# Deferred last tile between target groups of the graph attention loop, and rows B and C of the state space stage fetched in one transfer

## The chip, the cores and the metric

The kernel runs on one core of one Trainium2 chip. The metric is device microseconds of that core from start to end of one execution; "before" is the median of three runs. A profiled execution gives the trace that is read below. Engines are TensorE (PE, with its weight loads PEld), VectorE (DVE), ScalarE (ACT), GpSimd (POOL) and SyncE (SP), which only issues transfers.

## The reference, cut to what matters

Four layers of a graph network on 3125 nodes with 256 features. Layers 1 and 2 each hold a graph attention network of two attention layers; layer 3 holds one, and beside it a state space model (Mamba) over the nodes in sorted order. Of all this the change touches two parts. The second attention layer of layers 1 and 2 (and, of layer 1, the first too) is

```python
h = (x @ W).reshape(n, heads, out_ch)
e = leaky_relu(alpha_src[src] + alpha_dst[dst], 0.2)
m = segment_max(e, dst)
e = exp(e - m[dst])
alpha = e / segment_sum(e, dst)[dst]
out = segment_sum(alpha[:, :, None] * h[src], dst)
```

and its result, plus a bias, is added to x and normed over the features for the feed-forward part that follows. The state space model is a recurrence over the nodes with 16 states for each of 256 channels:

```python
dbc = xc @ x_proj_w.T                    # 16 values for dt, then rows B (16), then rows C (16)
dt = softplus(dbc[:, :16] @ dt_proj_w.T + dt_proj_b)
dA = exp(dt[:, :, None] * A);  dBx = (dt * xc)[:, :, None] * B[:, None, :]
h = dA_t * h + dBx_t                     # one step for each node t
y_t = h @ C_t
```

## The kernel before, in words

Nodes lie in 25 tiles of 125 (P) on the partitions. The program is written in a tile framework: the code says what is computed in which program order, the framework orders each engine's instructions by its own estimate of when their inputs are ready, and puts in the waits. So the code's order is a strong hint and not a list. [...]

**Attention.** `gat` (L1050) chooses between two ways; on these inputs `gat_products` (L1070) runs. It takes the targets in 5 groups (NG) of 5 tiles (GB). For a group, `spread` (L168) lays a factor of the targets along the free dimension: one-column transposes on TensorE into PSUM, copied out by ScalarE or VectorE (L78, L80). Then it goes over the 25 source tiles: a block of the dense adjacency is loaded by SyncE (`load_edges`), VectorE forms the weights `t` (L1124, one instruction for each head, three buffers), and TensorE adds `t`-block times `h` into one PSUM accumulator for each target tile and head (L1129). After the last source it calls `use` for each of the 5 target tiles in turn (L1132 and L1133) and runs it through before the next group's spreads are issued.

`use` is a generator of the caller. In `gat_last` (L1310; one head, width 256; layers 1 and 2) it is `use2`: divide by the sum of weights (`shares`, L1217: L1234, L1236, L1247 on VectorE), two additions on GpSimd (L1321, L1322), and after the fifth tile of a group the norm of all five (`centred`, L1799: statistics and a reciprocal root on VectorE with one step on ScalarE, then five scalings on ScalarE, L1806) and their turn (`turn`, L144: ten transposes on TensorE at L149 with four copies out on ScalarE at L151). In `gat_heads` (L1274; four heads) it is `use1`: shares, bias, ELU, transposes of the tile (L1299), copy out, a product with the next weights (L166), copies out. With width 128 (layer 1) `gat_heads` uses this loop too, with 7 PSUM banks for the accumulators and 1 for everything else. With width 64 (layers 2 and 3) another loop, `sums_by_feature`, runs, which the change leaves alone.

**State space.** `l3_mamba` (L1931) takes groups of four tiles (500 nodes), six of them and one of a single tile. `first_part` of a group makes xc, dt and u = dt * xc, and rows B and C. It is a generator, advanced one step for each state of the group before. A second generator, `beside`, runs layer 3's mixer (`l3_mix`), one step for each of the first nine states of a group. `recur(s)` handles state s for 128 channels at a time (c = 0, 1): the decay on ScalarE into PSUM (L2059), u times row B on VectorE (L2060), the scan along the nodes on VectorE (L2061), the last column kept on ScalarE (L2063), times row C on GpSimd (L2064). `add` sums the 16 states on TensorE with the identity (L2070); its buffer `bx` has four copies. Row B reaches the 128 partitions by a matmul (L2052): the 32 rows of B and C are split into three bfloat16 parts (`b1`, `b2`, `bc`; L2030 to L2038) and a one-column selection, broadcast, times them gives row s on all partitions, in PSUM. Row C comes by a transfer issued from ScalarE's queue: all C rows are written once for each group to DRAM (`crows`, L2033), and for each state one row is read back onto 128 partitions (L2049, three buffers).

Of the kernel before, what the change touches and what calls it, by code (L numbers as in the profile page):

```python
# [11 lines left out]
F32 = mybir.dt.float32  # L12
# [48 lines left out]
class Net:  # L61
# [1008 lines left out]
    def gat_products(self, far, h, al, heads, width, loops, use):  # L1070
# [3 lines left out]
        with ExitStack() as es:  # L1074
# [23 lines left out]
            cp = es.enter_context(self.pool("gq_acc", 1, PSUM))  # L1098
            pp = es.enter_context(self.pool("gq_ps", min(2, 8 - banks), PSUM))
            for g in range(NG):  # L1100
                rows = lp.tile([P, heads, GW], F32, name="rows")
# [14 lines left out]
                for s in range(NT):  # L1116
# [9 lines left out]
                    for b in range(GB):  # L1126
                        for hd in range(heads):
                            first = (b * heads + hd) % per == 0
                            nc.tensor.matmul(acc(b, hd), t[:, hd, b * P:(b + 1) * P], h[:, s, hd, :],  # L1129
                                             start=(s == 0 and first), stop=(s == NT - 1),  # L1130
                                             skip_group_check=True)
# [799 lines left out]
    def l3_mamba(self, xs, ys, beside):  # L1931
# [6 lines left out]
        with ExitStack() as es:  # L1938
# [20 lines left out]
            nc.vector.memset(state, 0.0)  # L1959

            wbc = wp.tile([128, KC, 3, 2 * S], F32, name="wbc")
            nc.vector.tensor_copy(wbc, wx[:, :, None, S:].to_broadcast([128, KC, 3, 2 * S]))
            pick = wp.tile([6 * S, 2 * S], BF16, name="pick")
            rest = wp.tile([6 * S, 2], F32, name="rest")
            for k in range(3):
                ks = slice(k * 2 * S, (k + 1) * 2 * S)
                nc.vector.tensor_copy(pick[ks], self.ident[ks, ks])
                for c in range(2):
                    nc.vector.memset(rest[ks, c:c + 1], float(k > c))
            crows = self.dram.tile([S, N], F32, name="crows")  # L1970
            last = wp.tile([128, KC, 3], F32, name="last")
            nc.vector.memset(last, 0.0)

            def first_part(g, n, into):
# [42 lines left out]
                for c in range(KC):  # L2017
# [8 lines left out]
                b1 = kp.tile([6 * S, 4 * P], BF16, name="b1", tag="b", bufs=1)  # L2026
                r1 = kp.tile([6 * S, 4 * P], F32, name="r1", bufs=1)
                b2 = kp.tile([6 * S, 4 * P], BF16, name="b2", tag="b", bufs=1)
                bc = kp.tile([6 * S, 4 * P], BF16, name="bc")
# [12 lines left out]
                nc.gpsimd.tensor_mul(u[:, :, :w], dt[:, :, :w], xc[:, :, :w])  # L2042
                into += [sz, xc, bc, dt, u]

            def recur(s, g, w, bc, dt, u):
# [6 lines left out]
                nc.tensor.matmul(bps[:, :w], pick[:, s:s + 1].to_broadcast([6 * S, 128]), bc[:, :w],  # L2052
                                 start=True, stop=True)
                out = []
                for c in range(KC):
# [3 lines left out]
                    nc.scalar.activation(da[:, :w], dt[:, c, :w], AF.Exp, scale=an[:, c, s:s + 1])  # L2059
                    nc.vector.tensor_mul(bx[:, :w], u[:, c, :w], bps[:, :w])  # L2060
                    nc.vector.tensor_tensor_scan(h[:, :w], da[:, :w], bx[:, :w], state[:, c, s:s + 1],  # L2061
# [28 lines left out]
            for k, (g, n) in enumerate(GROUPS):  # L2090
                w = n * P
                sz, xc, bc, dt, u = now
# [3 lines left out]
                terms = [recur(0, g, w, bc, dt, u)]  # L2096
                if done:
                    next(done)
                for s in range(S):
                    if s + 1 < S:  # L2100
                        terms.append(recur(s + 1, g, w, bc, dt, u))
                    if s:
# [21 lines left out]
    def l3_gnn(self):  # L2124
# [420 lines left out]
```

## Time and profile before

| what | us |
|---|---|
| median of three runs | 7015.29 (7009.70 to 7022.92) |
| profiled execution | 7013.64 |
| its span in the trace | 7011.9 |
| stretch with `gat_heads` of layer 1 | about 1781 to 2480 |
| stretch with `gat_last` of layer 1 | about 2480 to 2850 |
| stretch with `gat_last` of layer 2 | about 4375 to 4765 |
| stretch of the state space stage | about 5118 to 5826 |

Over the whole span TensorE is busy 85%, VectorE 53%, ScalarE 23%, GpSimd 13%. These are averages over stages with different limits, so the views below are taken by stage. A row of groups ends with the idle time just ahead of the group on its engine and the instruction that ended most of it. A row of the timeline has the start, the length, the engine, the line and the operation, and in brackets the idle time before it. A row of waits has the total, the number of times and the longest. In a table of stretches each engine has its busy time, then come the granted TensorE clock as a share of full speed, the share of the DMA engines and GB/s.

### The profile page before, as it was taken

Reading aid. Unit: us, or ns where it says so; the run is one execution under the profiler, and the core shown is the slowest. Engines: PE = TensorE matmul, PEld = TensorE weight load, DVE = VectorE, ACT = ScalarE, POOL = GpSimd, SP = SyncE. Lnnn points to the kernel's source line nnn. Section 1 sums busy time; section 2 is a strip of 40 time slices with the busy share of each in tenths; the row PEclk is TensorE's granted clock in tenths of the full one; section 3 lists DMA queues with packets and bytes.
Section 4 is the critical chain, followed back from the end, with each engine's and each line's share of the span. In section 5 each row is a group of like instructions: output and inputs, shape, how many; then the busy total and the mean of one; then the engine's idle time right before and its main releaser. Section 6 shows DMA issues by size and latency. Waiting matters only on the chain. (4 is left out here: it accounts for less than half of the span.)

```text
span 7011.9 us, 78426 instructions
## 1 busy us (share of the span) xinstructions
PE 5946.1 (85%) x29487; PEld 3981.8 (57%) x29487; DVE 3714.8 (53%) x7628; ACT 1603.4 (23%) x3404; POOL 885.3 (13%) x685
## 2 busy tenths in 40 slices
PE   6887999996799987899946999789878887998875
PEld 5555775664799966658843344676534333333543
DVE  7644123227776643215036887446377777776523
ACT  2423002331100010113313011001256661003411
POOL 0000000004000001400041000101324442001111
PEclk7978999998999998889977999898889998998887
DMA  2724447301122133315520322440232213222042
GB/s 67 109 40 71 129 133 229 98 9 61 53 62 60 53 105 102 92 50 174 174 59 15 82 78 55 114 115 9 79 40 55 58 45 89 65 70 75 31 120 79
DMA packets 421339, 562.00 MB, mean 80 GB/s; under 512 B 120485, under 2 KB 307169, under 8 KB 417153
## 3 DMA queue, kind: packets, MB, share of 16 engines
q1 hardware_dynamic: 353687, 458.72, 25.3%
q10 hardware_dynamic: 40467, 70.52, 3.7%
q0 software_dynamic: 26752, 27.20, 1.5%
q8 instruction: 247, 4.05, 0.2%
q14 instruction: 186, 1.52, 0.1%
HBM read 446.41 MB, written 109.65 MB: 79 GB/s over the span
## 5 line engine op out<-in xcount | busy, mean ns | idle before, releaser
L1124 DVE SCALAR_TENSOR_TENSOR t<-rows,over,a 125x625 f32<-125x625 f32 x750 | 617.4, 867 | 424.1 <-PE acc L1129 421.5
L1190 DVE SCALAR_TENSOR_TENSOR t<-rows,over,a 125x750 f32<-125x750 f32 (+1 forms) x800 | 795.0, 1045 | 57.8 <-PE acc L1204 53.3
L1195 PE MATMUL acc<-t,g_h 125*64 125x375 f32 (+1 forms) x3200 | 625.8, 500 | 12.2 <-DVE t L1190 12.2
L1129 PE MATMUL acc<-h,t 125*125 125x257 f32 x2500 | 566.4, 391 | 28.5 <-DVE t L1124 20.2
L1129 PE MATMUL acc<-g_h,t 125*125 125x129 f32 x5000 | 565.7, 275 | 1.3 <-DVE t L1124 1.1
L1129 PEld LDWEIGHTS acc<-g_h,t 125*125 125x125 f32 x5000 | 562.4, 189 | 3.2 <-DVE t L1124 2.9
L1129 PEld LDWEIGHTS acc<-h,t 125*125 125x125 f32 x2500 | 483.2, 194 | 110.5 <-issue 17.5
L1195 PEld LDWEIGHTS acc<-t,g_h 125*64 125x64 f32 x3200 | 226.9, 136 | 356.2 <-issue 247.0
L1204 PE MATMUL acc<-t,g_h 125*32 125x375 f32 (+1 forms) x3200 | 377.4, 497 | 0.0
L2064 POOL TENSOR_TENSOR bx<-h,crow 128x500 f32<-128x500 f32 (+1 forms) x224 | 270.6, 1223 | 343.1 <-DVE h L2061 107.2
L2070 PE MATMUL y<-bx,ident 128*128 128x500 f32 (+1 forms) x448 | 242.3, 650 | 76.7 <-POOL bx L2064 74.4
L771 PE MATMUL agg<-h,a 125*125 125x257 f32 x1250 | 278.0, 383 | 13.9 <-DMA a<-adj 8.7
L837 DVE SCALAR_TENSOR_TENSOR X<-ps_out,prob,X 125x256 f32<-125x256 f32 x200 | 87.9, 480 | 357.3 <-PE ps_out L166 357.1
L771 PEld LDWEIGHTS agg<-h,a 125*125 125x125 f32 x1250 | 233.4, 188 | 56.8 <-issue 18.1
L149 PE MATMUL ps_turn<-ident,XN 125*128 125x125 f32 x300 | 70.7, 386 | 223.9 <-DVE XN L138 109.8
L2061 DVE TENSOR_TENSOR_SCAN h<-da,state,bx 128x500 f32<-128x500 f32 (+1 forms) x224 | 246.9, 1130 | 20.7 <-ACT da L2059 17.8
L1204 PEld LDWEIGHTS acc<-t,g_h 125*32 125x32 f32 x3200 | 104.1, 109 | 249.6 <-issue 248.7
L563 ACT ACTIVATE h<-ps_hidden,L_ffn_b,bn_s 128x500 f32<-128x500 f32 (+1 forms) x224 | 160.6, 722 | 355.1 <-PE ps_hidden L166 330.7
L166 PE MATMUL ps_hidden<-xbt,w 128*128 128x250 f32 x928 | 204.6, 378 | 16.2 <-ACT xbt L151 16.2
L166 PE MATMUL ps_out<-w,hb 128*125 128x256 f32 x928 | 205.0, 379 | 0.0
L166 PE MATMUL ps_hidden<-XNT,L_ffn_W 128*128 128x500 f32 (+1 forms) x448 | 199.2, 569 | 0.0
L166 PEld LDWEIGHTS ps_hidden<-xbt,w 128*128 128x128 f32 x928 | 174.5, 191 | 41.9 <-ACT xbt L151 23.1
(724 smaller groups left out, 9477.3 us busy)
## 6 DMA issues: line engine op xcount, KB each, us to landing
a<-adj SPq DMA_DIRECT2D x500, 273.4 KB
a<-adj SPq DMA_DIRECT2D x150, 328.1 KB
arow<-adj SPq DMA_DIRECT2D x25, 1367.2 KB
adj<-block SPq DMA_DIRECT2D x22, 1531.2 KB
w<-in_L_ffn_W1p SPq DMA_DIRECT2D x29, 1024.0 KB
w<-in_L_ffn_W2p SPq DMA_DIRECT2D x29, 1024.0 KB
crow<-crows ACTq DMA_DIRECT2D x96, 250.0 KB
a<-adj SPq DMA_DIRECT2D x50, 382.8 KB
```

What stands on the lines that cost most here:

```text
L166: self.nc.tensor.matmul(ps, lhsT[k], rhs[k], start=(k == 0), stop=(k == n - 1))
L563: self.nc.scalar.activation(out[:, f, :], ps[:, :nt], func, **kw)
L771: nc.tensor.matmul(acc[b][:P, :D + 1], a[:, b * P:(b + 1) * P], h[:, s, :], start=(s == 0), stop=(s == NT - 1))
L837: nc.vector.scalar_tensor_tensor(x, ps, prob[:, g + j, e:e + 1], x, op0=ALU.mult, op1=ALU.add)
L1124: nc.vector.scalar_tensor_tensor(t[:, hd, :], rows[:, hd, :], over[:, s, hd:hd + 1], a, op0=ALU.max, op1=ALU.mult)
L1129: nc.tensor.matmul(acc(b, hd), t[:, hd, b * P:(b + 1) * P], h[:, s, hd, :], start=(s == 0 and first), stop=(s == NT - 1), skip_group_check ...
L1190: nc.vector.scalar_tensor_tensor(t[hd][:, :w], rows[hd][:, :w], over[:, s, hd:hd + 1], a[:, :w], op0=ALU.max, op1=ALU.mult)
L1195: nc.tensor.matmul(acc[k][c][q * width:(q + 1) * width, :c1 - c0], h[:, s, 2 * k + q, :width], t[2 * k + q][:, c0:c1], start=(s == 0), sto ...
L1204: nc.tensor.matmul(acc[pairs][c][hd * 32:(hd + 1) * 32, :c1 - c0], h[:, s1, hd, width:].to_broadcast([P, 32]), t1[hd][:, c0:c1], start=(s1 ...
L2061: nc.vector.tensor_tensor_scan(h[:, :w], da[:, :w], bx[:, :w], state[:, c, s:s + 1], op0=ALU.mult, op1=ALU.add)
L2064: nc.gpsimd.tensor_mul(bx[:, :w], h[:, :w], crow[:, :w])
L2070: nc.tensor.matmul(acc[c][:, :w], self.ident, terms[c][:, :w], start=(s == 0), stop=(s == S - 1))
```

## The change

In `gat_products` the `use` of a group's last tile is run only to its first yield; its remaining steps are taken one after every fourth source of the next group, and what is left is run before that group's own tiles. `use2` gets two yields, so its steps are: shares and additions; the norm; the first turn (three tiles); the second turn (two tiles). `use1` had its yields already (within the ELU, and between the copy out and the product).

In `l3_mamba` the rows B and C are computed once in float32, written together to DRAM as 32 rows (`bc_rows`), and for each state one transfer brings row B and row C onto 128 partitions. The split into bfloat16 parts, the selection tiles and the matmul for row B go. The PSUM pool of this function has one buffer in place of two, and the mixer's, `m3_ps`, three in place of two. Lines of the new kernel that answer to the old: L1125 to L1124, L1130 to L1129, L2037 to L2049, L2045 to L2059, L2046 to L2060, L2047 to L2061, L2049 to L2063, L2050 to L2064, L2056 to L2070.

```diff
@@ gat_products
+            later = iter(())
             for g in range(NG):
...
+                    if s % 4 == 3 and later:
+                        next(later, None)
+                self.through(later)
                 for b in range(GB):
-                    self.through(use(pp, g * GB + b, parts(b), None))
+                    later = use(pp, g * GB + b, parts(b), None)
+                    next(later, None)
+                    if b < GB - 1:
+                        self.through(later)
+            self.through(later)
@@ gat_last, use2
                 nc.gpsimd.tensor_add(self.X[:, i, :], self.X[:, i, :], x)
+                yield
                 if i % GB == GB - 1:
                     g = i - GB + 1
                     self.centred(kp, xn[:, g:g + GB, :], self.X[:, g:g + GB, :], GB, "li")
                     for b0, n in ((0, 3), (3, 2)):
+                        yield
                         self.turn(pp, xnt[:, :, (g + b0) * P:(g + b0 + n) * P], xn[:, g + b0:g + b0 + n, :], n,
                                   evac=nc.scalar.copy)
@@ l3_mamba
-            pp = es.enter_context(self.pool("mb_ps", 2, PSUM))
+            pp = es.enter_context(self.pool("mb_ps", 1, PSUM))
...
-            crows = self.dram.tile([S, N], F32, name="crows")
+            rows = self.dram.tile([2 * S, N], F32, name="bc_rows")
@@ l3_mamba, first_part
-                self.product(ps[:6 * S, :w], [wbc[:, c].rearrange("p k s -> p (k s)") for c in range(KC)],
-                             [xc[:, c, :w] for c in range(KC)])
...
-                nc.scalar.copy(b1[:, :w], ps[:6 * S, :w])
+                self.product(ps[:2 * S, :w], [wx[:, c, S:] for c in range(KC)], [xc[:, c, :w] for c in range(KC)])
                 both = kp.tile([2 * S, 4 * P], F32, name="both", tag="low", bufs=1)
                 nc.scalar.copy(both[:, :w], ps[:2 * S, :w])
-                nc.scalar.dma_start(crows[:, g * P:g * P + w], both[S:, :w])
-                nc.vector.scalar_tensor_tensor(r1[:, :w], b1[:, :w], rest[:, 0:1], ps[:6 * S, :w],
-                                               op0=ALU.mult, op1=ALU.subtract)
+                nc.scalar.dma_start(rows[:, g * P:g * P + w], both[:, :w])
                 yield
-                nc.scalar.copy(b2[:, :w], r1[:, :w])
-                nc.vector.scalar_tensor_tensor(bc[:, :w], b2[:, :w], rest[:, 1:2], r1[:, :w],
-                                               op0=ALU.mult, op1=ALU.subtract)
@@ l3_mamba, recur
-                crow = vp.tile([128, 4 * P], F32, name="crow")
-                row = crows[s:s + 1, g * P:g * P + w]
-                nc.scalar.dma_start(crow[:, :w], bass.AP(tensor=row.tensor, offset=row.offset,
-                                                         ap=[[0, 128], [1, w]]))
-                bps = pp.tile([128, 512], F32, name="ps_b", tag="mm")
-                nc.tensor.matmul(bps[:, :w], pick[:, s:s + 1].to_broadcast([6 * S, 128]), bc[:, :w],
-                                 start=True, stop=True)
+                both = vp.tile([128, 2, 4 * P], F32, name="both")
+                row = rows[s:s + 1, g * P:g * P + w]
+                nc.scalar.dma_start(both[:, :, :w], bass.AP(tensor=row.tensor, offset=row.offset,
+                                                            ap=[[0, 128], [S * N, 2], [1, w]]))
+                brow, crow = both[:, 0, :], both[:, 1, :]
...
-                    nc.vector.tensor_mul(bx[:, :w], u[:, c, :w], bps[:, :w])
+                    nc.vector.tensor_mul(bx[:, :w], u[:, c, :w], brow[:, :w])
@@ l3_gnn
-                pp = es.enter_context(self.pool("m3_ps", 2, PSUM))
+                pp = es.enter_context(self.pool("m3_ps", 3, PSUM))
```

More of the change, by code (lines that the diff above doesn't have):

```diff
@@ L1959, in l3_mamba @@
             nc.vector.memset(state, 0.0)
[L1961 to L1969, printed above, removed]
-            crows = self.dram.tile([S, N], F32, name="crows")
+            rows = self.dram.tile([2 * S, N], F32, name="bc_rows")
             last = wp.tile([128, KC, 3], F32, name="last")
@@ L2023, in first_part @@
                 ps = pp.tile([128, 512], F32, name="ps_dbc", tag="mm")
-                self.product(ps[:6 * S, :w], [wbc[:, c].rearrange("p k s -> p (k s)") for c in range(KC)],
-                             [xc[:, c, :w] for c in range(KC)])
[L2026 to L2029, printed above, removed]
-                nc.scalar.copy(b1[:, :w], ps[:6 * S, :w])
+                self.product(ps[:2 * S, :w], [wx[:, c, S:] for c in range(KC)], [xc[:, c, :w] for c in range(KC)])
                 both = kp.tile([2 * S, 4 * P], F32, name="both", tag="low", bufs=1)
                 nc.scalar.copy(both[:, :w], ps[:2 * S, :w])
-                nc.scalar.dma_start(crows[:, g * P:g * P + w], both[S:, :w])
-                nc.vector.scalar_tensor_tensor(r1[:, :w], b1[:, :w], rest[:, 0:1], ps[:6 * S, :w],
-                                               op0=ALU.mult, op1=ALU.subtract)
+                nc.scalar.dma_start(rows[:, g * P:g * P + w], both[:, :w])
                 yield
-                nc.scalar.copy(b2[:, :w], r1[:, :w])
-                nc.vector.scalar_tensor_tensor(bc[:, :w], b2[:, :w], rest[:, 1:2], r1[:, :w],
-                                               op0=ALU.mult, op1=ALU.subtract)
                 yield from self.softplus(fp, dt[:, :, :w], dt[:, :, :w])
@@ L2042, in first_part, with recur @@
                 nc.gpsimd.tensor_mul(u[:, :, :w], dt[:, :, :w], xc[:, :, :w])
-                into += [sz, xc, bc, dt, u]
-            def recur(s, g, w, bc, dt, u):
-                crow = vp.tile([128, 4 * P], F32, name="crow")
-                row = crows[s:s + 1, g * P:g * P + w]
-                nc.scalar.dma_start(crow[:, :w], bass.AP(tensor=row.tensor, offset=row.offset,
-                                                         ap=[[0, 128], [1, w]]))
-                bps = pp.tile([128, 512], F32, name="ps_b", tag="mm")
-                nc.tensor.matmul(bps[:, :w], pick[:, s:s + 1].to_broadcast([6 * S, 128]), bc[:, :w],
-                                 start=True, stop=True)
+                into += [sz, xc, dt, u]
+            def recur(s, g, w, dt, u):
+                both = vp.tile([128, 2, 4 * P], F32, name="both")
[3 more added lines that the diff above has]
+                brow, crow = both[:, 0, :], both[:, 1, :]
                 out = []
@@ L2091, in l3_mamba @@
                 w = n * P
-                sz, xc, bc, dt, u = now
+                sz, xc, dt, u = now
                 now = []
@@ L2095, in l3_mamba @@
                 acc = [cp.tile([128, 512], F32, name=f"y{c}") for c in range(KC)]
-                terms = [recur(0, g, w, bc, dt, u)]
+                terms = [recur(0, g, w, dt, u)]
                 if done:
@@ L2100, in l3_mamba @@
                     if s + 1 < S:
-                        terms.append(recur(s + 1, g, w, bc, dt, u))
+                        terms.append(recur(s + 1, g, w, dt, u))
                     if s:
```

## The prediction

> **What bounds the kernel now.** The change touches two kinds of stage, so I read each stage by itself: first the costliest groups (line, engine, operation, tile, count | busy us, mean ns | idle before, and who ended it).
>
> ```profile
> L1124 DVE SCALAR_TENSOR_TENSOR t<-rows,over,a 125x625 f32<-125x625 f32 x750 | 617.4, 867 | 424.1 <-PE acc L1129 421.5
> L1129 PE MATMUL acc<-h,t 125*125 125x257 f32 x2500 | 566.4, 391 | 28.5 <-DVE t L1124 20.2
> ```
>
> In the source loop of `gat_products` VectorE waits for TensorE (421.5 us), hardly the reverse: TensorE sets the pace. Its own holes lie between groups of targets. The timeline of TensorE about one boundary in `gat_last` of layer 1:
>
> ```profile
> 2689.72 11.22 PE L1129 MATMUL acc<-h,t 125*125 125x257 f32 x51
> 2710.74 1.66 PE L149 MATMUL ps_turn<-ident,XN 125*128 125x125 f32 x6 [9.80 <-ACT XN L1806]
> 2713.06 1.09 PE L149 MATMUL ps_turn<-ident,XN 125*128 125x125 f32 x4 [0.66 <-ACT XNT L151]
> 2714.20 1.41 PE L174 MATMUL ps_spread<-ident,mine 125*125 125x125 f32 x5
> 2717.08 3.36 PE L1129 MATMUL acc<-h,t 125*125 125x257 f32 x7 [1.47 <-DVE t L1124]
> ```
>
> The products end at 2700.94 and start again at 2717.08: a hole of 16.1 us, nearly all of it the norm of the five tiles (9.80 us of waiting) and their turns. The other boundaries of both `gat_last` stages show the same within 0.3 us. The products also come back slow. The stretches table (us, busy of PE, PEld, DVE, ACT, POOL, granted clock, DMA):
>
> ```profile
> 2717.00:2722.00 5.00, 4.92 (x12) 3.87 (x13) 1.82 (x4) 0.00 (x0) 0.00 (x0) 0.50 0.68 188
> ```
>
> One source takes 2.17 us in steady state (VectorE's next `t` starts every 2.17 us); the first after the hole takes 4.69 (2717.08 to 2721.77). So a hole costs about 2.5 us more.
>
> The state space stage runs from about 5118 to 5822. Its waits (us in total, times, longest) and four stretches:
>
> ```profile
> PEld y L2070 <- POOL bx L2064: 157.1, 121, 4.1
> POOL bx L2064 <- DVE h L2061: 107.1, 38, 12.4
> DVE bx L2060 <- PE ps_b L2052: 67.6, 22, 16.7
> ```
> ```profile
> 5300.00:5310.00 10.00, 10.00 (x29) 5.12 (x28) 4.51 (x6) 4.15 (x10) 2.20 (x2) 1.00 0.18 51
> 5310.00:5320.00 10.00, 10.00 (x38) 6.79 (x37) 5.26 (x12) 6.50 (x12) 1.97 (x3) 1.00 0.07 26
> 5340.00:5350.00 10.00, 7.62 (x27) 3.59 (x26) 10.00 (x14) 6.05 (x12) 5.78 (x4) 1.00 0.22 45
> 5350.00:5360.00 10.00, 6.54 (x18) 2.89 (x18) 10.00 (x10) 6.00 (x13) 4.08 (x3) 0.91 0.16 46
> ```
>
> A group of four tiles (some 105 us) has two halves: first TensorE is full with the mixer that runs beside it and VectorE waits for row B, which stands in TensorE's queue; then VectorE is full. By the scans' starts, some 43 of the 96 steps of full width (one state each) take under 5.3 us, the shortest 3.47: there VectorE is the bound. The rest take longer.
>
> **What the Trainium skill says.** "SBUF — State Buffer", Who interferes with whom: VectorE with two inputs in SBUF and a GpSimd instruction that reads SBUF exclude each other for a whole instruction; an input in PSUM takes VectorE out of this. The trace agrees:
>
> ```profile
> 5457.23 3.39 POOL L2064 TENSOR_TENSOR bx<-h,crow 128x500 f32<-128x500 f32 x2 [1.35 <-DVE h L2061]
> ```
> ```profile
> 5458.18 1.35 DVE L1926 SCALAR_TENSOR_TENSOR sp_l<-sp_w,sp_l 128x1000 f32<-128x1000 f32 x1
> 5460.04 1.65 DVE L1927 TENSOR_TENSOR sp_l<-sp_l,sp_z 128x1000 f32<-128x1000 f32 x1
> ```
>
> Two of GpSimd's products take 2.46 us undisturbed and 3.39 here; L1927 takes 1.20 alone (at 5151.6) and 1.65 here. L2060, with B in PSUM, is never over 0.68. "TensorE: Matmul & The Clock Gate", Part 1: after an idle window of about 3.4 us the array runs at half rate until it has been busy for as long; the 0.50 above agrees. On a transfer's cost the trace serves: a `crow` of 250 KB has its first packet 1.0 us after issue and the last about 2.0 us later.
>
> **Part 1: `gat_last`, 2 stages x 4 boundaries.** The last tile's shares and its two GpSimd additions stay; norm and turns move behind sources 4, 8 and 12 of the next group. In the new instruction order the spreads follow the last product at once, VectorE's first `t` stands between the fourth and fifth tile's shares, and the turns stand seven or more sources in. In the old trace the fourth share ends at 2703.72 and the fifth at 2705.20; with `t` at 0.87 the products can start at about 2705.0, a hole of 4.0 (up to 5.7, if `t` comes after the fifth share and the 0.42 copy of rows). Removed: 16.1 - 4.0 = 12.1. What is late next is that share chain. Added to TensorE's full stream: ten transposes, 2.75 us at half rate here, taken as 2.0 (1.2 to 2.75). Clock: with a hole of 4 us I take half of the 2.5 us back, 1.2 (0 to 2.5). VectorE's moved norm, about 4.5 us, lies in its 1.3 us of idle per source with three `t` ahead, ScalarE's part in an idle engine; it issues no transfer, so SyncE's loads are not touched; if VectorE's lead ran out it would cost up to 2 us a boundary. Net 12.1 - 2.0 + 1.2 = 11.3; x8 = **90 us** (61 to 107).
>
> **Part 2: `gat_heads` of layer 1, 4 boundaries.** Only its width of 128 comes through this loop. One tile of five takes 3.84 us at the boundary (5 such steps up to 1919.63), of which 2.66 is TensorE's (0.65 + 2.01) and goes into the next group's full stream at some 2.2: 1.6 x4 = **6 us** (5 to 9). The single PSUM buffer is free between, as turn and product stand four sources apart.
>
> **Part 3: state space.** Gains: the 67.6 us of VectorE waiting for B. Now it may run as far as `bx`'s four buffers allow, and next it waits for TensorE's sums (L2070), in the same full queue; I take half, 34. The 112 products for B hold TensorE 0.22 us each (5304.82 to 5305.04), 25 us, half of them where TensorE is full: 12. L2034 and L2038, 0.72 + 0.83 us x7 on VectorE: 11. Sum 57 (11 to 104). `mb_ps` falls to one buffer and `m3_ps` rises to three: taken as nothing, since the products for B used those turns; a few us either way.
> Losses: L2060's time hardly changes by itself (a two-input operation on 512 elements from SBUF, L1294, takes 0.68), but it now locks out GpSimd. In a step bound by VectorE two scans (2.40), two products (1.23 overlapped) and GpSimd's two (2.46) meet: the first product comes 0.3 us before GpSimd's first ends; the second may meet all of GpSimd's second, 1.24. So 0.3 to 1.5 per step; I take 1.0 for 45 such steps: 45 us. The transfer doubles to 500 KB, some 5 us to landing by the above; ScalarE issues it only when GpSimd is done with the buffer three steps before (behind that wait stand state copies and exponentials, as now). New is that L2060 waits for the transfer; behind it on VectorE stand its own scans and the mixer's norms, and GpSimd and TensorE's sums wait for those. Ring: 5.3 + 1.23 + 2.40 + 1.3 = 10.2 us for three steps, 3.4 each: within a step's 3.47 to 5.3. In the last, short group (16 steps near 1.5 to 2 us) the ring is the longer: some 6 us. First rows: 2. Sum 53 (20 to 152).
> Net **4 us** gained (from 84 gained to 141 lost).
>
> **Sum.** Span 7011.9, the profiled execution 7013.6; 7013.6 - 90 - 6 - 4 = 6913.6. The median, 7015.3, lies 1.7 above it: **6915 us**.
>
> **Rivals.** (a) Row B was what held the stage: all 67.6 and 25 us come back and GpSimd's lock falls mostly into slack: 55 further, 6860. For: 16.7 us single waits. Against: the sums stand in the same queue. 17%. (b) The lock costs 1.5 in each step bound by VectorE and little of the wait returns: about 65 lost there, 6980. For: the alternation in the trace. 20%. (c) The moved steps don't close the hole, a quarter comes back: 6990; the order of instructions speaks against. 6%. (d) Slower: each of the 96 steps pays 1.5 us of the lock, 144, since VectorE is then the bound throughout, with 8 for the short group and only 23 returned: 7015 - 96 + 129 = 7048. It decides from 1.16 us net per step. Against: where TensorE is full, VectorE has half its time free. 6%. The forecast, 6885 to 6945: 51%.
>
> **Numbers.** 0.2%, 14 us, is about what can be told from no change. The range reaches over most of (a) and (b): 6855 to 6985. Faster: 51 + 17 + most of (b) and (c), 0.90; same 0.04; slower 0.06.
>
> **What would show it.** Right: holes of 4 to 6 us before the products of L1130, ten transposes within the stream; no wait for B on TensorE; `bx<-u,both` well over 0.66 us on average and GpSimd's product over 1.35. Wrong: holes over 10 us; waits of VectorE for `both` by DMA over 30 us; the state space stage longer than before by over 50 us.

## The result, and the profile after

The changed kernel takes 6972.62 us (median of six runs, 6965.84 to 6983.80), the kernel before, on the same chip, 7013.89: a ratio of 0.9942, 95% interval 0.9929 to 0.9955, a gain of 41 us. The forecast was 6915. The profiled execution took 6965.84, its span is 6964.0, so it can be set against the span of 7011.9 of before.

Where the 48 us between the spans come from is read by landmarks, taken from the timelines of TensorE and VectorE: the starts of the same instructions in both traces.

| stretch | before | after | gained | forecast |
|---|---|---|---|---|
| `gat_heads` of layer 1, first product to last | 680.8 | 675.7 | 5 | 6 |
| `gat_last` of layer 1, first product of group 1 to first of group 5 | 292.1 | 238.3 | 54 | 45 |
| `gat_last` of layer 2, the same | 290.8 | 238.3 | 52 | 45 |
| state space: last `ps_kv` row of the timeline to the first scan | 65.6 | 87.2 | -22 | -2 |
| state space: first scan to last | 657.8 | 701.2 | -43 | +6 |

So by these landmarks the attention part gained 111 where 96 was forecast, and the state space part lost 65 where a gain of 4 was forecast. The two `gat_last` stretches end before the turns of their last deferred tile; to the last product of each stage the gains are 53 and 51, so the attention part gained 109 in all.

**Attention.** TensorE's timeline over the boundary of groups 4 and 5 of `gat_last` in layer 1 (start, length, then what):

```profile
2698.08 28.35 PE L1130 MATMUL acc<-h,t 125*125 125x257 f32 x130
2730.20 19.27 PE L1130 MATMUL acc<-h,t 125*125 125x257 f32 x80 [3.23 <-DVE t L1125]
2749.30 0.80 PE L149 MATMUL ps_turn<-ident,XN 125*128 125x125 f32 x6
```

The hole is 3.8 us (the first row ends at 2726.43, the products return at 2730.20) in place of 16.1; the six transposes of the first turn stand eight sources on, between products. The clock, in stretches (busy PE, PEld, DVE, ACT, POOL, then the granted clock, DMA share, GB/s):

```profile
2726.00:2730.00 4.00, 0.98 (x7) 0.73 (x6) 3.06 (x11) 0.47 (x1) 3.77 (x6) 1.00 0.01 2
2730.00:2735.00 5.00, 4.80 (x15) 3.90 (x16) 4.38 (x11) 0.00 (x0) 4.84 (x5) 0.66 0.55 146
```

The first stretch after the hole has 0.66 where it had 0.50. Eighty products take 17.58 to 19.27 us after a hole of 3.8 us and 17.68 in steady state (twice 8.84), so such a hole costs 0 to 1.6 us more. By the same measure a hole of before costs 1.5 to 2.9 us more (19.14 to 20.62 in layer 2); the 2.5 of the forecast came from one of the costliest.

**State space.** Three groups of before, and the three that answer to them after:

```profile
L2060 DVE TENSOR_TENSOR bx<-u,ps_b 128x500 f32<-128x500 f32 (+1 forms) x224 | 129.4, 605 | 72.3 <-PE ps_b L2052 67.6 <-PE y L2070 3.6 <-POOL u L2042 1.1
L2064 POOL TENSOR_TENSOR bx<-h,crow 128x500 f32<-128x500 f32 (+1 forms) x224 | 270.6, 1223 | 343.1 <-DVE h L2061 107.2
L2070 PE MATMUL y<-bx,ident 128*128 128x500 f32 (+1 forms) x448 | 242.3, 650 | 76.7 <-POOL bx L2064 74.4
```
```profile
L2050 POOL TENSOR_TENSOR bx<-h,both 128x500 f32<-128x500 f32 (+1 forms) x224 | 282.5, 1277 | 350.5 <-DVE h L2047 134.9
L2056 PE MATMUL y<-bx,ident 128*128 128x500 f32 (+1 forms) x448 | 257.5, 694 | 117.0 <-POOL bx L2050 112.3
L2046 DVE TENSOR_TENSOR bx<-u,both 128x500 f32<-128x500 f32 (+1 forms) x224 | 205.8, 947 | 39.4 <-DMA both<-bc_rows 33.5
```

VectorE's product by row B took 129 us in all before (605 ns each) and takes 206 now (947 ns); TensorE's sums wait 112 us for GpSimd in place of 74. The wait for B on TensorE (67.6) is gone, and in its place stand 33.5 us for the transfer.

The product is not slower by itself. Of the 192 products of full width in the trace of after, 80 overlap no GpSimd instruction and take 667 ns on average (680 at most), as before the change (667); the other 112 overlap one and take 1296 on average, up to 2775. Before, with row B in PSUM, 129 overlapped one and none took over 675. In all, the products of after are 70 us longer than 192 times 667 ns: 42 of it in the first eight states of the groups and 29 in the last eight.

One place where the two engines meet, from the timelines of GpSimd and of VectorE:

```profile
5507.35 3.39 POOL L2050 TENSOR_TENSOR bx<-h,both 128x500 f32<-128x500 f32 x2 [3.54 <-issue]
5510.70 2.73 POOL L2030 TENSOR_TENSOR u<-dt,xc 128x1000 f32<-128x1000 f32 x1
```
```profile
5508.29 1.35 DVE L1939 SCALAR_TENSOR_TENSOR dt<-dt,sp_l 128x1000 f32<-128x1000 f32 x1
5509.57 4.39 DVE L2046 TENSOR_TENSOR bx<-u,both 128x500 f32<-128x500 f32 x2
```

Two products that take 1.25 us undisturbed take 4.39, and end half a microsecond after GpSimd's `u` does. The eight longest single products (2.76 to 2.78 us) all do the same: each starts 0.50 us after a GpSimd operation of the size of `u` and ends 0.53 us after it.

**The start of the stage.** This loss was not in my sum. ScalarE, TensorE and VectorE ahead of the first scan, each from its timeline:

```profile
5030.25 0.37 ACT L1840 COPY y<-ps_out 125x256 f32<-125x256 f32 x1 [0.27 <-PE ps_out L166]
5048.34 0.34 ACTq L2026 DMA_DIRECT2D bc_rows<-both  x1
5048.71 1.28 ACT L1933 ACT_TABLE_LOAD   x1 [18.09 <-DMA pk_m<-mask]
```
```profile
5051.56 1.10 PE L1984 MATMUL ps_turn<-ident,x 125*128 125x125 f32 x4 [20.88 <-ACT xt L1986]
5067.55 2.03 PE L166 MATMUL ps_in<-xt,L_gnn_in_proj_w 128*128 128x500 f32 x2 [14.89 <-ACT xt L1986]
```
```profile
5063.69 0.87 DVE L2235 TENSOR_TENSOR pk_full<-pk_m,g_al 125x400 f32<-125x400 bf16 x1 [9.89 <-DMA pk_m<-mask]
5064.48 1.19 DVE L1939 SCALAR_TENSOR_TENSOR dt<-dt,sp_l 128x1000 f32<-128x1000 f32 x1
```

As the stage begins, SyncE loads 32 pieces of mask columns (`pk_m`, issued from 5004.55 to 5060.04; in 5030 to 5055 alone SyncE's queue moves 23,769 packets for 0.05 MB, two bytes each). ScalarE's issue of the rows' write stands for 18 us with the end of one of these loads as its releaser, and a copy that TensorE waits for (`xt`) stands behind it; the next such copy stands behind exponentials that wait for `dt`.

Why the issue stands is in the semaphores of the trace. The program lets the transfers of SyncE and of ScalarE signal their landing on the same eight semaphores in turn, and an issue first waits until the transfer before it on its own semaphore has landed. The write's semaphore had last gone to a mask load that SyncE issued only at 5044.08, 14 us after the rows were ready (5029.98). That load landed at 5048.26, the write was issued at 5048.34 and landed at 5051.58, 3.2 us later. So the burst's packets cost the write little (in kernel 8 below, which has no mask loads, it lands 1.6 us after its issue); it is its place in the turn of the semaphores that costs the 18.

And on VectorE the softplus's last step (`dt`, L1939), which everything after needs, stands behind `pk_full`, which needs all the mask columns: the inputs of `dt` are ready at 5053.71, and the first scan starts at 5069.94. In the trace of before `dt` ran first, and `pk_full` among the scans:

```profile
5153.01 1.19 DVE L1929 SCALAR_TENSOR_TENSOR dt<-dt,sp_l 128x1000 f32<-128x1000 f32 x1
```
```profile
5189.22 0.87 DVE L2249 TENSOR_TENSOR pk_full<-pk_m,g_al 125x400 f32<-125x400 bf16 x1
```

### The profile page after: what moved, and what is told of

Its sections match the earlier page's. It is cut to its first block, busy times and chain, and to the rows that moved or that the text cites. A ratio compares the mean times of both kernels' runs of the same rounds, so it can differ in the third digit from the quotient of the medians.

```text
span 6964.0 us, 78182 instructions
## 1 busy us (share of the span) xinstructions
PE 5918.7 (85%) x29375; PEld 3966.3 (57%) x29375; DVE 3784.7 (54%) x7604; ACT 1590.8 (23%) x3385; POOL 916.2 (13%) x685
## 5 line engine op out<-in xcount | busy, mean ns | idle before, releaser
L1125 DVE SCALAR_TENSOR_TENSOR t<-rows,over,a 125x625 f32<-125x625 f32 x750 | 621.5, 871 | 395.9 <-PE acc L1130 395.2
L1203 PE MATMUL acc<-t,g_h 125*64 125x375 f32 (+1 forms) x3200 | 625.8, 500 | 12.9 <-DVE t L1198 12.9
L1130 PE MATMUL acc<-h,t 125*125 125x257 f32 x2500 | 559.1, 385 | 28.9 <-DVE t L1125 26.4
L1130 PE MATMUL acc<-g_h,t 125*125 125x129 f32 x5000 | 571.5, 276 | 1.6 <-DVE t L1125 1.4
L1130 PEld LDWEIGHTS acc<-g_h,t 125*125 125x125 f32 x5000 | 567.9, 190 | 3.4 <-DVE t L1125 3.2
L1130 PEld LDWEIGHTS acc<-h,t 125*125 125x125 f32 x2500 | 473.5, 190 | 108.1 <-issue 20.3
L2056 PE MATMUL y<-bx,ident 128*128 128x500 f32 (+1 forms) x448 | 257.5, 694 | 117.0 <-POOL bx L2050 112.3
L2050 POOL TENSOR_TENSOR bx<-h,both 128x500 f32<-128x500 f32 (+1 forms) x224 | 282.5, 1277 | 350.5 <-DVE h L2047 134.9
L2047 DVE TENSOR_TENSOR_SCAN h<-da,state,bx 128x500 f32<-128x500 f32 (+1 forms) x224 | 246.5, 1130 | 29.2 <-ACT da L2045 24.4
L2056 PEld LDWEIGHTS y<-bx,ident 128*128 128x128 f32 x448 | 87.9, 231 | 248.3 <-POOL bx L2050 211.7
L2046 DVE TENSOR_TENSOR bx<-u,both 128x500 f32<-128x500 f32 (+1 forms) x224 | 205.8, 947 | 39.4 <-DMA both<-bc_rows 33.5
```

The lines of the kernel that those rows point to most:

```text
L1125: nc.vector.scalar_tensor_tensor(t[:, hd, :], rows[:, hd, :], over[:, s, hd:hd + 1], a, op0=ALU.max, op1=ALU.mult)
L1203: nc.tensor.matmul(acc[k][c][q * width:(q + 1) * width, :c1 - c0], h[:, s, 2 * k + q, :width], t[2 * k + q][:, c0:c1], start=(s == 0), sto ...
L2046: nc.vector.tensor_mul(bx[:, :w], u[:, c, :w], brow[:, :w])
L2050: nc.gpsimd.tensor_mul(bx[:, :w], h[:, :w], crow[:, :w])
L2056: nc.tensor.matmul(acc[c][:, :w], self.ident, terms[c][:, :w], start=(s == 0), stop=(s == S - 1))
```

## The experiments

Theory L, from these traces: attention gained about 113; the state space part lost about 65, of it 43 in the scans by the lock between VectorE and GpSimd, and 22 at the start. The rivals: the single PSUM buffer (P), the wait for the transfer (D). All times are medians; the ratio is to the kernel before on the same chip, and where times of different chips are compared it is the better guide (0.001 is 7 us). The two columns on the right are from each trace: from the last `ps_kv` row to the first scan, and from the first scan to the last. Kernels with the same state space part agree within 6 us in the scans (656.9 to 658.6, 699.3 to 705.5), so less than that is not read as a difference. Some expectations speak of halves: the first half of a group runs from the scan of state 0 to that of state 8, the second from there to the next group's first scan, summed over the six full groups. Before they are 334 and 292 us, in the changed kernel 296 and 371, and the short group has 32 and 34.

| kernel | us | ratio, 95% interval | to first scan | scans |
|---|---|---|---|---|
| before | 7013.89 | | 65.6 | 657.8 |
| changed | 6972.62 | 0.9942 [0.9929, 0.9955] | 87.2 | 701.2 |
| 1 deferred tile alone | 6910.96 | 0.9847 [0.9834, 0.9861] | 65.1 | 658.6 |
| 2 state space part alone | 7077.98 | 1.0087 [1.0073, 1.0101] | 87.5 | 705.5 |
| 3 changed, PSUM pools as before | 6961.68 | 0.9915 [0.9902, 0.9929] | 68.0 | 709.9 |
| 4 changed, B copied into PSUM | 6930.46 | 0.9871 [0.9856, 0.9886] | 88 | 661.3 |
| 5 changed, product reads xc | 6948.55 | 0.9906 [0.9891, 0.9921] | 87 | 688.2 |
| 6 changed, product reads da | 6888.10 | 0.9822 [0.9809, 0.9835] | 88.2 | 620.1 |
| 7 half of the states by transfer | 6932.57 | 0.9878 [0.9863, 0.9893] | 70.5 | 676.3 |
| 8 changed, no mask columns | 6944.93 | 0.9897 [0.9882, 0.9913] | 58.5 | 699.3 |
| 9 changed, GpSimd writes the rows | 6952.45 | 0.9908 [0.9893, 0.9923] | 86.5 | 686.9 |
| 10 as 1, no mask columns | 6894.15 | 0.9832 [0.9816, 0.9847] | 52.7 | 656.9 |
| 11 as 9, `dt` ahead of `pk_full` | 6942.37 | 0.9892 [0.9877, 0.9907] | 72.4 | 687.0 |
| 12 as 1, GpSimd writes the rows | 6902.52 | 0.9838 [0.9824, 0.9851] | 62.1 | 657.1 |

In 4 and 5 the last `ps_kv` row lacks records, so its start is corrected by 0.43 us for each missing product.

**1 and 2: each half of the change alone.** The edits of one half are taken back: `l3_mamba` and the mixer's pool in the first, `gat_products` and `use2` in the second.

> The deferred tile alone, state space stage and its PSUM pools as before. Theory L (the attention part gained about 113 us and the state space part lost about 65, mostly by the lock between VectorE and GpSimd): 7014 - 113 = about 6901. Rival (my terms for attention were right, 96 us, and the trace's shift is partly something else): about 6918.

> The state space part alone (rows B and C by one transfer, the two PSUM pools), attention as before. Theory L: 7014 + 65 = about 7079, of which about 22 stand ahead of the first scan and about 43 in the scans. Rival (the state space loss comes only in company with the deferred tile, as a shift of a transfer burst): the 22 are absent, about 7057. My forecast's own value: 7010.

Measured: 6911 and 7078; by the ratios -107 us (-116 to -97) and +61 us (51 to 71). The interval of the first holds theory L's 113 and leaves the rival's 96 just outside. The halves add: 0.9847 x 1.0087 = 0.9933, inside the interval of the whole change. The start of the stage is as late in the second kernel (87.5) as in the changed one, so it doesn't come from the company of the deferred tile. Theory L holds for both parts, and the deferred tile alone is faster than both kernels.

**3: the PSUM pools as before.**

```diff
-            pp = es.enter_context(self.pool("mb_ps", 1, PSUM))
+            pp = es.enter_context(self.pool("mb_ps", 2, PSUM))
-                pp = es.enter_context(self.pool("m3_ps", 3, PSUM))
+                pp = es.enter_context(self.pool("m3_ps", 2, PSUM))
```

> The changed kernel with the two PSUM pools as before (two buffers each). Theory L (lock and the blocked ScalarE queue): the scans stay as long as in the changed kernel, about 701 us from first to last, and at most the 22 us ahead of the first scan return: 6951 to 6973. Rival P (the single PSUM buffer of the state space function makes TensorE wait for ScalarE's copies throughout): half or more of the 65 us returns, 6940 or less.

Measured: 19 us of the start return (68.0), the scans don't (709.9); in all 11 us by the medians, 19 by the ratios. Rival P falls for the scans. For the start it holds through the order: with two buffers the framework puts `dt` ahead of `pk_full` on VectorE (5054.80 against 5083.83). All six kernels above with one buffer and no other remedy (changed, 2, 4, 5, 6, 9) have `pk_full` first, all with two (before, 1, 3, 7) have `dt` first. It is `mb_ps` that decides: kernel 4 has the mixer's pool at two again, and `pk_full` is still first.

**4: the transfer stays, the lock goes.**

```diff
-                brow, crow = both[:, 0, :], both[:, 1, :]
+                crow = both[:, 1, :]
+                brow = bp.tile([128, 512], F32, name="brow")
+                nc.scalar.copy(brow[:, :w], both[:, 0, :w])
```

> The changed kernel with row B copied by ScalarE from the fetched rows into one PSUM bank (taken from the mixer's pool, two buffers there), so that VectorE's product has one input in SBUF again: no lock, but the transfer and its wait stay, and ScalarE gets 112 copies of some 0.56 us. Theory L: the second halves of the groups fall back by most of their 79 us, the time to about 6900 to 6925. Rival D (the wait for the transfer is what costs): no faster than 6965, since the chain transfer, copy, product is longer by 0.6 us per step.

Its groups:

```profile
L2049 DVE TENSOR_TENSOR bx<-u,brow 128x500 f32<-128x500 f32 (+1 forms) x224 | 128.7, 610 | 88.1 <-ACT brow L2042 86.0 <-PE y L2059 2.1
L2042 ACT COPY brow<-both 128x500 f32<-128x500 f32 (+1 forms) x112 | 59.5, 531 | 48.7 <-DMA both<-bc_rows 26.4 <-DVE bx L2049 20.5 <-DVE h L2050 1.3
```

Measured: 6930, 42 us faster than the changed kernel (50 by the ratios), 40 of it in the scans (661.3), though VectorE now waits 86 us for the copy. Theory L's 6900 to 6925 is missed by 5 us: the second halves fall by 39 us (332), half of the 79. A longer chain behind the transfer, and yet faster: rival D can't be the main cause.

**5 and 6: VectorE doesn't wait for the transfer; the lock stays in 5 and goes in 6.** The first added line is kernel 5's, the second kernel 6's.

```diff
-                    nc.vector.tensor_mul(bx[:, :w], u[:, c, :w], brow[:, :w])
+                    nc.vector.tensor_mul(bx[:, :w], u[:, c, :w], xc[:, c, :w])
+                    nc.vector.tensor_mul(bx[:, :w], u[:, c, :w], da[:, :w])
```

> The changed kernel with VectorE's product reading another SBUF tile of the same size (xc, ready long before) in place of row B: row B's values are left out of the result, its transfer stays. VectorE still has two inputs in SBUF and so the lock, but waits for no transfer. Theory L (lock): second halves of the groups stay near the changed kernel's 371 us (355 or more) and the time within 15 us of its 6973. Rival D (VectorE's wait for the transfer, 33 us in sum, and what hangs on it): 40 us or more return, about 6930.

> The changed kernel with VectorE's product reading the decay da, which stands in PSUM, in place of row B (row B's values left out, its transfer stays): neither lock nor wait for the transfer, and no extra copy. Theory L: second halves back to about 292 us as before the change, first halves near 296 or below, the time about 6973 - 79 = 6894. Rival D: no different from the run with xc in place of row B.

The groups of full width, GpSimd's product and VectorE's, of kernel 5 and of kernel 6:

```profile
L2050 POOL TENSOR_TENSOR bx<-h,both 128x500 f32<-128x500 f32 x192 | 271.1, 1424 | 319.1 <-DVE h L2047 117.1 <-issue 60.0 <-PE y L2056 30.3
L2046 DVE TENSOR_TENSOR bx<-u,xc 128x500 f32<-128x500 f32 x192 | 187.2, 1000 | 28.0 <-PE y L2056 21.5 <-POOL u L2030 6.5
```
```profile
L2050 POOL TENSOR_TENSOR bx<-h,both 128x500 f32<-128x500 f32 x192 | 249.5, 1313 | 278.0 <-DVE h L2047 133.3 <-issue 43.5 <-PE y L2056 41.7
L2046 DVE TENSOR_TENSOR bx<-u,da 128x500 f32<-128x500 f32 x192 | 123.8, 663 | 44.7 <-ACT da L2045 42.9 <-PE y L2056 1.6
```

The same operation on the same shape takes 1000 ns with both inputs in SBUF and 663 with one in PSUM; GpSimd's takes 1424 and 1313. From the scans: 701.2 to 688.2 for the wait on the transfer (13 us), 688.2 to 620.1 for the lock (68 us), and 620.1 against 657.8 of before is what taking row B off TensorE is worth where neither the lock nor the transfer is paid for (38 us). So 5, at 6949 us, lies between its two theories (within 15 of 6973, or about 6930), and its second halves, 335 us, fell below theory L's 355 while its first rose to 315: the wait for the transfer is real, a fifth of the lock's size. Kernel 6 has theory L's time (6888 for 6894), and rival D falls, but by another split than expected: the second halves didn't fall to 292 (327); the gain shows in the first (259). These two kernels also differ in the framework's order on VectorE, so 68 is the two things together. The decay `da` is waited for in both, 37 us at the scan in 5 and 46 at the product in 6. That VectorE's own busy time on this line differs by the same 68 (200.3 against 132.4 over both widths) speaks for the lock.

**7: row B by transfer only where TensorE is full.**

```diff
+                if s < 8:
+                    row = rows[s:s + 1, g * P:g * P + w]
...
+                else:
+                    row = rows[S + s:S + s + 1, g * P:g * P + w]
...
+                    nc.tensor.matmul(brow[:, :w], pick[:, s:s + 1].to_broadcast([6 * S, 128]), bc[:, :w],
+                                     start=True, stop=True)
```

> The deferred tile, and in each group of the state space stage states 0 to 7 take row B by the transfer and states 8 to 15 by TensorE's product into PSUM as before (the bfloat16 split stays; a temporary of the softplus and one of the split share other tiles' places). Theory L: the same edit gains where TensorE is full (38 us over the first halves) and loses where VectorE is (79 over the second), so this has the gain alone: 6911 - 38 = about 6873, first halves near 296 us, second near 292. Rival S (both are one balance, and what is gained in the first half comes back as waiting in the second): about 6911, the same as with the deferred tile alone.

Measured: 6933, slower than with the deferred tile alone by some 22 us, and slower than either theory. First halves 347 us (334 before), second 297. My reading of the halves was wrong. In the changed kernel the first eight states of a group are quick and the last eight slow partly because waiting moves from one to the other, as it does without any lock in kernel 6 (259 and 327 for 334 and 292). Here the first eight states run ahead of TensorE and meet its queue in one piece, as a step of 17 to 24 us from state 7 to 8 in four of the six full groups:

```profile
5346.51 3.52 PE L166 MATMUL ps_q<-x,L_mix_Wq 128*128 128x500 f32 x8
5349.86 0.38 PE L2071 MATMUL ps_b<-bc,pick 96*128 96x500 bf16 x1
```

The product for state 8 stands behind the mixer's, VectorE's (at 5350.28) behind it. The lock is paid for half of the states (900 ns for a full product on average), and nothing is won. That these steps are the cause is not shown: of the 18 us that the scans lose against kernel 1, 8 fall in the first group, which has no such step, and kernel 1 has single steps of up to 20 us too. The places that two temporaries share in this kernel are a rival that no run tests.

**8 and 10: without the mask columns,** in the changed kernel and with the deferred tile alone.

```diff
-            d = nc.values_load(at[0:1, k:k + 1], engines=[mybir.EngineType.SP], min_val=0, max_val=N - 1)
-            for part in (slice(0, EVEN), slice(EVEN, P)):
-                nc.sync.dma_start(edges[part, k, :], rows[part, :, bass.ds(d, 1)].rearrange("p s o -> p (s o)"))
+            nc.gpsimd.memset(edges[:, k, :], 0.0)
```

> The changed kernel without the 32 loads of mask columns (some 51,000 packets of 12 bytes) that run as the state space stage begins; the columns are set to zero, so that part of the result is left out. Theory M (ScalarE's transfer issues stand behind that burst, 18.1 us, and VectorE behind its end, 9.9): the first scan comes 25 us or more earlier after the start of the stage, about 6945. Rival P (the single PSUM buffer by itself makes the start longer): at most 5 us return, about 6970.

(The 12 bytes counted another load of the same queue with it; the packets have two.)

> The deferred tile alone, without the 32 loads of mask columns (set to zero, so that part of the result is left out). Theory M (the burst costs the changed kernel some 28 us because of how its order meets it, and the order of before much less): from the run with the deferred tile alone, 6911, some 5 to 10 us come off, about 6903. Rival (the burst costs every order the same): 28 us, about 6883.

Measured: in the changed kernel the first scan comes 28.7 us sooner (58.5) and the time falls by as much (28 us by the medians, 32 by the ratios); the scans stay (699.3). Theory M holds there, and rival P falls. In the other order it is 12.4 us (65.1 to 52.7) at the start; the time falls by 17 by the medians, 11 by the ratios, whose intervals overlap. So the mask loads cost both, the changed kernel some 16 more at the start; the theory's 5 to 10 for the order of before was too low.

**9 and 11: which of the two waits at the start matters.** Kernel 9 has the first diff, kernel 11 both (the `gate` line follows the softplus).

```diff
-                nc.scalar.dma_start(rows[:, g * P:g * P + w], both[:, :w])
+                nc.gpsimd.dma_start(rows[:, g * P:g * P + w], both[:, :w])
```
```diff
+                self.gate = dt
...
         full = pool.tile([P, K, NT], F32, name="pk_full")
+        nc.gpsimd.tensor_copy(full[:, 0, 0:1], self.gate[:P, 0, 0:1])
```

> The changed kernel with the 32 rows of each group written to DRAM from GpSimd's queue in place of ScalarE's. Theory Q (what hurts is that ScalarE's copies and softplus stand behind its own blocked issue): ScalarE's 18.1 us of waiting and TensorE's two waits of 20.9 and 14.9 us behind it go, and most of the 22 us ahead of the first scan return, about 6952. Rival R (the rows are simply late, whoever issues them, and VectorE still waits for the end of the burst): the first scan comes at most 5 us earlier, 6968 or more.

> As the run with GpSimd's write, and VectorE's work on the mask columns held back by a one-element copy until a late group's dt is there, so that dt of the first group no longer stands behind it on VectorE. Theory O (the order on VectorE sets the first scan: dt waits 26.6 us behind the end of the burst): the first scan comes some 14 us earlier, bounded then by the first rows' arrival (reads issued at 5051 in the run with GpSimd's write, some 5 us to landing), the time about 6938. Rival (rows are late anyway, the scan starts no earlier): about 6952.

Kernel 9 has the time that theory Q named, 6952, for another reason. ScalarE's wait of 18.1 at the write and TensorE's of 20.9 and 14.9 behind it are gone, but the first scan is no earlier (86.5). The write now has a semaphore that no mask load uses. It is issued at 5033.03, 0.3 us after the rows are ready, and lands at 5035.16, amid the burst; of the seven such writes none takes over 5.7 us:

```profile
L2026 POOL DMA_DIRECT2D bc_rows<-both x7: 525/542/849, 5033.0 to 5698.2; - x7
DMA to landing us min/median/max: 1.9/2.3/5.7
```

(The first row has the shortest, median and longest time of the issue in ns, and the first and last start.) The first read of the rows is issued 16 us later all the same:

```profile
5051.26 0.91 ACTq L2037 DMA_DIRECT2D both<-bc_rows  x2
```

It signals on one of the eight semaphores, and the mask load before it there landed at 5051.19. On VectorE the inputs of `dt` are ready at 5038.73:

```profile
5065.43 0.87 DVE L2235 TENSOR_TENSOR pk_full<-pk_m,g_al 125x400 f32<-125x400 bf16 x1 [26.61 <-DMA pk_m<-mask]
5066.22 1.19 DVE L1939 SCALAR_TENSOR_TENSOR dt<-dt,sp_l 128x1000 f32<-128x1000 f32 x1
```

VectorE reaches `pk_full` sooner and waits longer, and `dt` stands behind it for 27 us. The scans are 14 us shorter (686.9), perhaps because TensorE does work ahead of them in which it would have stood still; no run shows it. With `dt` put ahead:

```profile
5043.86 1.20 DVE L1939 SCALAR_TENSOR_TENSOR dt<-dt,sp_l 128x1000 f32<-128x1000 f32 x1
...
5061.38 1.27 DVE L2047 TENSOR_TENSOR bx<-u,both 128x500 f32<-128x500 f32 x2 [16.25 <-DMA both<-bc_rows]
5062.57 2.40 DVE L2048 TENSOR_TENSOR_SCAN h<-da,state,bx 128x500 f32<-128x500 f32 x2
```

the first scan comes 14 us sooner (72.4), as expected, and now waits for the rows: the write landed at 5040.89, but the first read is issued only at 5056.21, just after a mask load on its semaphore (5056.14). The order on VectorE set the start; theory O holds. (The whole times of 9 and 11, 6952 and 6942, have ratios whose intervals overlap.)

**12: the best version.** The deferred tile with the C rows' write moved to GpSimd (the same one line as in 9, for `crows`).

> The deferred tile alone with the C rows written from GpSimd's queue: the best version so far with the one edit of the start that paid. Theory Q (ScalarE's split of row B and softplus stand behind its own blocked issue, 7.9 us, in this order too): some 5 to 8 us off 6911, about 6904. Rival: the start is set by the arrival of the rows, no change, 6911.

Measured: 6902.52, 3 us sooner to the first scan. Against the deferred tile alone (ratio 0.9847) the intervals overlap, so it is not shown to be faster than that; by the ratios either beats both kernels, the one before by 107 to 114 us and the changed one by 67 to 73.

## Why the prediction was wrong

- **Part 1, `gat_last`: right in mechanism, low in size.** 104 us for 90, to the last product of each stage. The hole is 3.8 as forecast (4.0), at the first boundary of a stage only 1.7 in all, so 12.9 are removed on average for my 12.1; the ten transposes now stand among products and push them back by 1.1 us (0.64 and 0.43) for my 2.0; of the cold clock's cost, 2.1 us a hole on average before and about 1.0 now, 1.1 returned for my 1.2. 12.9 - 1.1 + 1.1 = 12.9, against 13.1 measured (104.4 / 8).
- **Part 2, `gat_heads`: right.** 5 us for 6.
- **Part 3 failed.** I put a net gain of 4; kernel 2 alone loses 61 us, and the landmarks say 65. The step that failed most is the lock's, which was counted only in the steps that VectorE bounds; next come the start of the stage, put at 2 and at nothing, and the gains. The terms, with what the runs put in their place:
  - Gains: "Sum 57", of it "I take half, 34", the TensorE slots 12 and the split 11. Kernel 6 has 38 in all.
  - "I take 1.0 for 45 such steps: 45". The lock costs 68 (kernel 5 against 6). The size per step was not far off; that it would be paid only in steps bound by VectorE was wrong. It lengthens the product wherever GpSimd is at work (0.66 to 1.03 us over all 192 full products; 58 of the 96 full steps pay, 37 of them in the first halves, where TensorE was full) and holds GpSimd's up in turn, on whose results TensorE's sums wait. Spread over 96 steps it is 0.7 each.
  - The transfer, "some 6 us" in the short group: 13 us on VectorE in all (changed against 5); the short group itself grew by 2 only (32.1 to 34.2). The 500 KB land 3.8 us after the issue (median of 112), sooner than my 5.
  - "First rows: 2" and "`mb_ps` falls to one buffer and `m3_ps` rises to three: taken as nothing": together 22 us. That is the largest error after the lock's, and it is one of order: the framework, given one buffer, put `pk_full` ahead of `dt` (14 of the 22, by kernel 11). The forecast followed the new order of instructions only around the attention boundaries.
  - In sum 38 - 68 - 13 - 22 = -65 for +4: errors of 19, 23, 7 and 20. That the sum closes proves nothing, since each term is the difference of two neighbours in the chain before, 6, 5, changed.
- **The rivals.** My (b), the lock at 1.5 a step with little of the wait returned, had about 65 lost there and 6980: near in sum, and in part by luck: 1.5 in some 45 steps is about the 68 measured, though other steps pay it, and the start, which it didn't have, makes up for what returned. Of the signs I named, the holes of 4 us, the transposes within the stream and the vanished wait for B on TensorE were right, as were the longer products of VectorE and of GpSimd (1.35 to 1.41 us for the full ones); of those for wrong, the wait for `both` over 30 us (33.5) and the stage longer by over 50 came.

The Trainium skill's "SBUF — State Buffer", Who interferes with whom, which the forecast used, is borne out and priced here: 663 against 1000 ns on average, 667 either way without a GpSimd instruction beside it. "DMA: Bandwidth & Descriptors", Issuing engines are not separate DMA queues, says that transfers from any engine run on the same DMA engines and interleave, and that another issuing engine saves only the time of the issue, usually small. What the traces show agrees: with GpSimd's issue the write lands in 2.1 us amid SyncE's burst, and the issue itself takes 0.34 us on ScalarE and 0.56 on GpSimd. The 18.1 us that ScalarE stood were a wait for a semaphore and not the issue, and 13.5 of them came back at its first read in kernel 9.

What stays open: how far the change of VectorE's order, apart from the lock, shares in the 68 us; where the scans' 14 us in kernel 9 were won; what slows kernel 7; and what a semaphore that no mask load shares would give to the reads of the rows as well as to their write, which no run tried.

## What to carry to other kernels

An operand that moves from PSUM to SBUF isn't free on VectorE, even when its own time in the profile is the same: count every GpSimd instruction that may run beside it, in all steps and not only in those that VectorE bounds. When a wait is shifted from one engine's queue to another's, ask of each half of a stage whether the work has gone or only moved; a half that gets quicker proves nothing. Where a framework orders the instructions, changing one pool by one buffer is a change of order: follow it on every engine up to the first instruction that all others need. And where an engine stands ahead of issuing a transfer, see which semaphore it waits for, and who else signals on it, before blaming the transfers in flight.

## What the runs showed that I had not expected

A burst of some 50,000 packets of two bytes on SyncE's queue, about 0.1 MB in 55 us, made ScalarE stand for 18 us ahead of the issue of a 62.5 KB write (8.5 in the kernel before), with all that stood behind that issue. It was not the packets: by its semaphore the write had to wait for a mask load, and issued from GpSimd on another semaphore it landed in 2.1 us amid the same burst. Without the loads the first scan came 28.7 us sooner in one order and 12.4 in another. And products of VectorE back to back beside GpSimd don't take turns evenly: 4.39 us for two, where 1.25 is their time alone.
